# The gates of a mixture of experts loaded from ScalarE's queue, one expert sooner, and constant rows filled for one head and copied by transfers

## The chip, the cores and the metric

The kernel runs on one core of a Trainium2 chip. The core has TensorE (PE, matrix products; PEld is its weight load), VectorE (DVE), ScalarE (ACT), GpSimd (POOL) and SyncE (SP), each with its own queue of instructions taken in order, and DMA engines that move data between HBM and the on-chip memory SBUF and within SBUF. A transfer is started by an instruction in some engine's queue; SP does nothing else in this kernel. The metric is the time of one launch on the device in microseconds (us), lower being better.

## The reference, cut to what matters

Four blocks follow each other on an input of 4 sequences of 1024 tokens of 128 channels, each as `x = x + layernorm(block(layernorm(x)))`: an RWKV layer, a mixture of 16 experts with a shared one, a DeltaNet (linear attention), and a grouped-query attention with a mixture of 8 experts. The change touches the second and prepares the fourth.

```python
# second block: 4 of 16 experts by grouped top-k, and a shared one
weights, idx = _gate(x, w_gate)
combine = (one_hot(idx, E) * weights[..., None]).sum(1)          # [tokens, 16]
g = silu(einsum('th,efh->tef', x, w1_e))
u = einsum('th,efh->tef', x, w3_e)
routed = einsum('tef,ehf,te->th', g * u, w2_e, combine)
return routed + swiglu_shared(x)

# third block, per head and token: state M (8x8) and Z (8), decayed by beta
M = M * b_t + k_t v_t^T;  Z = Z * b_t + k_t
y_t = (q_t M) / (q_t Z + eps)

# fourth block: 16 query heads, 4 key heads of 8 channels, causal
att = softmax(q k^T / sqrt(8)); h = x + (att v) wo; out = h + moe8(rmsnorm(h))
```

## The kernel before, in words

Channels stand on the 128 partitions and tokens along the free axis. A sequence is worked in two halves of `CH` = 512 tokens, so most operations have the shape 128x512. Three overlapping stretches make up the span:

- **0 to 303 us.** The RWKV layer (`time_mixing`, `channel_mixing`, up to L355), and from about 190 us the first experts beside it.
- **190 to 683 us.** Experts (`gates_b` L382, `stage_b` L453) and from 303 us the first two sequences' DeltaNet (`stage_c` L551). The order in which a Python loop calls them is `with_experts`: a step of the DeltaNet adds 0.28 (a scan step) or 0.1 to a counter, and one step of the experts is called whenever it passes 1. Before this point a scheduler of the framework decides the order on each engine from the program, its dependencies and its buffers, so a line that waits for something else may change the order of many others.
- **683 us to the end.** Attention, the 8 experts and the DeltaNet of the last two sequences. Their order is written out by hand (`tc.manual_schedule()` near the end of the program).

**Experts.** Two experts of 64 hidden channels fill 128 partitions, so 16 experts are 8 pairs; from here "expert" means such a pair. For each half, `stage_b` goes through `[8 (shared), 0, 1, ..., 7]`. `begin(j)` issues: a product into PSUM; on DVE `x` = that, bounded below (L472); on ACT Exp, Ln, Exp, which make the sigmoid `g` (L474 to L476); for j < 8 the load of the gate and on POOL `x * gate` (L481); on POOL `g * x` (L482). Two experts later come the product `u_ps`, `g * u` on DVE (L492) and the product into `y_ps` (L465). The gates of a half are the rows of the combine weights, which `gates_b` computes on DVE (top-k) and writes to HBM (`rows`, L448). The load of an expert's gate (L480, on SP) reads its two rows from HBM and spreads each over 64 partitions: a tile 128x512 of 256 KB. Three buffers (`bufs=3`) hold gates, so the load of one waits until the multiply of the gate three back is done. There are 64 such loads (4 sequences, 2 halves, 8 experts).

**DeltaNet.** For each half `stage_c` loads the rotary table (`turn`, L570), computes `v`, writes it to HBM (`v_rows`, L582), makes `phi` for queries and keys (POOL `u` L599, DVE L603 and L610, ACT between), loads each value row spread over the partitions (`vrep`, L619, SP), multiplies it by the keys (POOL `kv`, L623), scans along time (DVE, L629, two scans for each of 9 rows), adds the two states (POOL `qs`, L639) and multiplies by the queries (DVE, L643). At the end POOL adds the result to the stream `xT` (L713).

**Attention's tiles.** `keys_r` (2 tiles, 2 halves x 4 heads of 512) and `queries_r` (2 tiles, 16 heads of 512) are bfloat16, heads along the free axis. Rows 0 to 71 are filled for each half by `spread` (L893) with 18 transfers (L901, L905) from `dk` and `dq` in HBM, where `heads` (L846) has written them (L883). Rows 64 to 127 hold constants first: -1 for keys, 0 for queries. Four memsets on POOL write them (L824, L825), in the program text just behind the first sequence's DeltaNet.

The lines that the change and the steps of the prediction touch most are `begin` in `stage_b` and the memsets.

Of the kernel before, what the change touches and what calls it, by code (L numbers as in the profile page):

```python
# [21 lines left out]
CH = 512  # L22
NH = T // CH
# [16 lines left out]
def sandwich(ctx: ExitStack, tc: tile.TileContext, x, vecs, cmats, rope, wa, wb, wc, wd, out):  # L40
# [3 lines left out]
    nc = tc.nc  # L44
# [69 lines left out]
    def chunk(h):  # L114
        return slice(h * CH, (h + 1) * CH)

    def rstd(var, eps, scale=1.0, to=None):

        r = var if to is None else to
        nc.scalar.activation(r, var, AF.Ln, bias=eps, scale=scale)  # L120
        nc.scalar.activation(r, r, AF.Exp, scale=-0.5)
        return r

    def mean_square(pp, src, bias=0.0):
        sq = pp.scratch("rs")
        nc.scalar.activation(sq, src, AF.Square, bias=bias)  # L126
        return project(pp, mean, sq, "ln_v")
# [8 lines left out]
    def project(pp, lhsT, rhs, name):  # L136
        ps = pp([P, CH], name)
        nc.tensor.matmul(ps, lhsT=lhsT, rhs=rhs, start=True, stop=True)  # L138
        return ps
# [313 lines left out]
    def stage_b(b, pp):  # L453

        n1, rows = ready_b.pop(b)
        pairs_of = rows.rearrange("(c e) k t -> c (e k) t", e=2)

        for h in range(NH):
            c = chunk(h)
            py = pp([P, CH], "y_ps")  # L460
            hid = []

            def add_up(last):
                w, a = hid.pop(0)
                nc.tensor.matmul(py, lhsT=w, rhs=a, start=(w is w2s), stop=last)  # L465

            def begin(j):


                pgate = project(pp, w1s if j == 8 else w1[:, j, :], n1[h], "g_ps")  # L470
                x = pb.tile([P, CH], FP, tag="x", name="x", bufs=3)
                nc.vector.tensor_scalar_max(x, pgate, -41.0)  # L472
                g = pb.tile([P, CH], FP, tag="g", name="g", bufs=4)
                nc.scalar.activation(g, x, AF.Exp, scale=-1.0)  # L474
                nc.scalar.activation(g, g, AF.Ln, bias=one)
                nc.scalar.activation(g, g, AF.Exp, scale=-1.0)  # L476
                if j < 8:

                    gate = pb.tile([P, CH], FP, tag="gate", name="gate", bufs=3)
                    nc.sync.dma_start(out=gate, in_=pairs_of[j][:, c].unsqueeze(1).to_broadcast([16, 8, CH]))  # L480
                    nc.gpsimd.tensor_mul(x, x, gate)  # L481
                nc.gpsimd.tensor_mul(g, g, x)  # L482
                return g

            begun = []
            for j in [8, 0, 1, 2, 3, 4, 5, 6, 7, None, None]:
                if j is not None:
                    begun.append((j, begin(j)))
                if len(begun) > 2 or j is None:
                    k, g = begun.pop(0)  # L490
                    pup = project(pp, w3s if k == 8 else w3[:, k, :], n1[h], "u_ps")
                    nc.vector.tensor_mul(g, pup, g)  # L492
                    hid.append((w2s if k == 8 else w2[:, k, :], g))
                if len(hid) > 1:
                    add_up(False)
                if j is not None:
                    yield
            add_up(True)
            rs = rstd(mean_square(pp, py), eps5, to=pp.scratch("rs"))
            nc.vector.tensor_mul(rs, py, rs)  # L500
            nc.gpsimd.tensor_add(xT[b][:, c], xT[b][:, c], rs)
            yield
# [224 lines left out]
    def experts_b(b):  # L727

        ahead = gates_b(b + 1, room_b) if b + 1 < NB else iter(())
        for n, _ in enumerate(stage_b(b, room_b)):  # L730
            if n in (3, 5) or 10 < n < 18:
                next(ahead, None)
            if n + 1 == 20:
                whole(ahead)
            yield
# [12 lines left out]
    while running or behind_a or coming_a:  # L748
        if coming_a and count >= BEHIND:
            b, h = coming_a[0]  # L750
# [5 lines left out]
        for item in list(running):  # L756
            kind, b, h, steps = item
# [63 lines left out]
    keys_r = [pk.tile([P, NH, 4, CH], BF, name=f"keys_r{i}") for i in range(2)]  # L821
    queries_r = [pe.tile([P, 16, CH], BF, tag=f"qr{i}", name=f"queries_r{i}", bufs=1) for i in range(NH)]
    for kr, qr in zip(keys_r, queries_r):
        nc.gpsimd.memset(kr[64:128], -1.0)  # L824
        nc.gpsimd.memset(qr[64:128], 0.0)  # L825

    def parts3(dst, src):

# [536 lines left out]
```

## Time and profile before

| | |
|---|---|
| median of 3 runs | 1573.81 us (1573.48 to 1579.96) |
| profiled execution | 1576.56 us, of it span 1574.8 us |
| mean granted TensorE clock | 0.892 |
| busy: PE / DVE / ACT / POOL | 78% / 68% / 54% / 53% |
| DMA engines | 59329 packets, 90.48 MB |

The profile is one execution as the hardware profiler saw it. Times in a timeline count from the start of the span. "L481" is line 481 of the kernel before; "x<-x,gate" says that tile x is written from x and gate. "SPq" is the queue of transfers on SP: a row of it is the issue of a transfer, not the transfer. In the timeline, brackets give the idle time ahead of an instruction on its engine, and what ended it. The granted clock is the share of its full speed that TensorE was given.

### The profile page before, as it was taken

The page shows a single profiled execution, that of the slowest core. Times are in us where ns is not written, and L with a number is a line of the kernel's source. Part 1 is how long each engine was busy: PE and PEld are TensorE (multiplying, and loading weights), DVE is VectorE, ACT ScalarE, POOL GpSimd, SP SyncE. Part 2 cuts the span into 40 slices and gives each one's busy share as a digit, 9 for nine tenths or more (in the row PEclk, how much of TensorE's full clock was granted, in tenths as well). Part 3 has the DMA queues.
Part 4 walks back from the last instruction along what each step waited for, and adds up shares of the span by engine and source line. Part 5 has one row for each costly group of instructions (what it writes and reads, how often), then busy time and mean ns, then how long its engine had stood idle before and what let it go on. Part 6 is the DMA issues. An engine that isn't in the chain of part 4 may idle for free.

```text
span 1574.8 us, 15028 instructions
## 1 busy us (share of the span) xinstructions
PE 1231.2 (78%) x4524; PEld 448.9 (29%) x4532; DVE 1064.7 (68%) x1755; ACT 849.2 (54%) x1565; POOL 842.2 (53%) x901
## 2 busy tenths in 40 slices
PE   3478889949878678888689778858977888989864
PEld 1123333313223223233223223312322333233211
DVE  4676775567864786876996896697479666577501
ACT  3566777544437445546445446534653474755541
POOL 5565485696838657953534653562556454223312
PEclk8677999968879789999889899988998999999986
DMA  2000020321223413201102111312121113111102
GB/s 105 14 14 0 14 69 32 73 72 48 93 40 98 137 40 100 67 28 59 50 30 87 50 42 44 103 49 74 56 83 38 57 38 105 44 59 45 57 24 61
DMA packets 59329, 90.48 MB, mean 57 GB/s; under 512 B 9904, under 2 KB 26800, under 8 KB 58544
## 3 DMA queue, kind: packets, MB, share of 16 engines
q1 hardware_dynamic: 59248, 89.52, 18.9%
q8 instruction: 36, 0.59, 0.2%
q14 instruction: 45, 0.37, 0.1%
HBM read 76.38 MB, written 12.71 MB: 57 GB/s over the span
## 4 chain that ended last, share of the span: by engine, by line
PE 35%; DVE 23%; ACT 7%; POOL 5%; issue 4%; SPq 2%; DMA 2%; POOLq 0%; DVEq 0%; ACTq 0%
DVE st L629 8%; PE av L992 7%; PE sc L1000 5%; DVE ms L936 4%; PE y L1131 3%; DVE ms L941 3%; PE ln_v L138 3%; PE sm L940 2%; PE sm L928 2%; ACT pr L1005 2%; PE g_ps L138 2%; DVE qs L643 2%; PE u_ps L138 1%; PE y_ps L465 1%; PE num_ps L680 1%
## 5 line engine op out<-in xcount | busy, mean ns | idle before, releaser
L1005 ACT ACTIVATE pr<-sc 128x512 f32<-128x512 f32 x576 | 328.4, 596 | 294.9 <-PE sc L1000 289.3
L936 DVE TENSOR_REDUCE ms<-sm 128x1 f32<-128x512 f32 (+3 forms) x352 | 212.3, 632 | 109.8 <-PE sm L932 101.7
L1000 PE MATMUL sc<-queries_r,keys_r 128*128 128x512 bf16 x576 | 224.6, 399 | 29.2 <-ACT pr L1005 27.6
L941 DVE TENSOR_REDUCE ms<-sm 128x1 f32<-128x512 f32 x256 | 166.0, 681 | 59.0 <-PE sm L940 58.9
L992 PE MATMUL av<-pr,va 128*32 128x512 f32 x1152 | 170.9, 652 | 4.2 <-POOL pr L1009 3.3
L928 PE MATMUL sm<-keys_r,queries_r 125*128 125x512 bf16 (+3 forms) x512 | 131.3, 313 | 44.9 <-DVE ms L936 37.1
L1009 POOL TENSOR_SCALAR_AFFINE_SELECT pr<-pr 128x512 f32<-128x512 f32 x128 | 95.4, 759 | 119.7 <-ACT pr L1005 119.0
L138 PE MATMUL ln_v<-rs,cm 128*128 128x512 f32 x176 | 110.1, 718 | 42.1 <-ACT rs L126 33.5
L1119 POOL TENSOR_TENSOR share<-n,every 128x512 f32<-128x512 f32 x64 | 80.6, 1273 | 99.5 <-DMA every<-row 58.5
L639 POOL TENSOR_TENSOR qs<-st,st 128x512 f32<-128x512 f32 x72 | 101.7, 1414 | 40.4 <-PE num_ps L680 15.6
L940 PE MATMUL sm<-keys_r,queries_r 125*128 125x512 bf16 x256 | 95.1, 395 | 22.8 <-DVE ms L941 19.5
L623 POOL TENSOR_TENSOR kv<-vrep,phi 128x512 f32<-128x512 f32 x64 | 86.7, 1357 | 41.7 <-issue 18.6
L481 POOL TENSOR_TENSOR x<-x,gate 128x512 f32<-128x512 f32 x64 | 84.0, 1314 | 46.7 <-ACT g L474 43.7
L482 POOL TENSOR_TENSOR g<-g,x 128x512 f32<-128x512 f32 x72 | 92.7, 1291 | 12.8 <-POOL x L481 6.7
L138 PE MATMUL g_ps<-n,wbt 128*128 128x512 f32 x144 | 83.8, 672 | 16.0 <-DVE x L472 7.5
L465 PE MATMUL y_ps<-g,wbt 128*128 128x512 f32 x144 | 79.7, 639 | 21.0 <-DVE g L492 20.6
L1000 PEld LDWEIGHTS <-keys_r 128*128 128x128 bf16 x576 | 57.5, 102 | 130.5 <-issue 101.5
L932 PE MATMUL sm<-later,identb 128*128 128x128 bf16 (+2 forms) x344 | 86.5, 251 | 0.0
L492 DVE TENSOR_TENSOR g<-u_ps,g 128x512 f32<-128x512 f32 x72 | 49.3, 685 | 54.7 <-POOL g L482 32.7
L138 PE MATMUL u_ps<-n,wbt 128*128 128x512 f32 x144 | 79.8, 638 | 1.7 <-DVE x L472 0.7
L928 PEld LDWEIGHTS <-queries_r 125*128 125x128 bf16 x512 | 48.6, 102 | 108.4 <-issue 91.5
L474 ACT ACTIVATE g<-x 128x512 f32<-128x512 f32 x72 | 45.0, 626 | 57.0 <-DVE x L472 56.9
(302 smaller groups left out, 2369.4 us busy)
## 6 DMA issues: line engine op xcount, KB each, us to landing
gate<-rows SPq DMA_DIRECT2D x64, 256.0 KB
vrep<-v_rows SPq DMA_DIRECT2D x64, 256.0 KB
every<-row SPq DMA_DIRECT2D x64, 256.0 KB
queries_r<-dq SPq DMA_DIRECT2D x72, 128.0 KB
turn<-in_rope_dram SPq DMA_DIRECT2D x8, 512.0 KB
dq<-qp SPq DMA_DIRECT2D x8, 384.0 KB
keys_r<-dk SPq DMA_DIRECT2D x72, 32.0 KB
sums<-av_sb SPq DMA_DIRECT2D x128, 18.0 KB
```

The source lines that it names most:

```text
L138: nc.tensor.matmul(ps, lhsT=lhsT, rhs=rhs, start=True, stop=True)
L465: nc.tensor.matmul(py, lhsT=w, rhs=a, start=(w is w2s), stop=last)
L629: nc.vector.tensor_tensor_scan(sts[e][i], beta[i], kvs[e], before if h else 0.0, op0=ALU.mult, op1=ALU.add,)
L639: nc.gpsimd.tensor_add(sums_e[e][0], s0, s1)
L928: nc.tensor.matmul(view[:, k, :], lhsT=qr[0:MROWS, h, tb], rhs=kr[0:MROWS, half, h // 4, 0:n_s], start=(k == 0), stop=False, skip_group_ch ...
L936: nc.vector.tensor_reduce(ms[:, 0, h0 : h0 + in_bank], view, AX.X, ALU.max)
L940: nc.tensor.matmul(sc, lhsT=qr[0:MROWS, h, tb], rhs=kr[0:MROWS, 0, h // 4, :], start=True, stop=True)
L941: nc.vector.tensor_reduce(ms[:, 1, h : h + 1], sc, AX.X, ALU.max)
L992: nc.tensor.matmul(pavs[b, i][32 * g : 32 * g + 32, :], lhsT=va[:, j, g, :], rhs=pr, start=(j == 0), stop=(j == i),)
L1000: nc.tensor.matmul(sc, lhsT=kr[0:ROWS, j // 4, g, j % 4 * P : (j % 4 + 1) * P], rhs=qr[0:ROWS, 4 * g : 4 * g + 4, tb], start=True, stop=True,)
L1005: nc.scalar.activation(pr, sc, AF.Exp)
L1009: nc.gpsimd.affine_select(out=every, in_=every, compare_op=ALU.is_ge, fill=0.0, base=0, pattern=[[0, 4], [1, P]], channel_multiplier=-1,)
```

## The change

1. The load of a gate moves from SP's queue to ACT's, and each expert loads the gate of the next one: the shared expert (8) loads that of expert 0, expert 0 that of expert 1, and so on; expert 7 loads none. The number of loads, their size and the number of buffers stay. A list `gates` carries the tile from one `begin` to the next.
2. The memsets fill rows 64 to 127 for one head only (64x512 in place of 64x4096 and 64x8192). Four transfers on SP copy this head to the other 15 query heads or 7 key heads, within SBUF.

```diff
                 if j < 8:
+                    nc.gpsimd.tensor_mul(x, x, gates.pop(0))
+                if j != 7:
 
                     gate = pb.tile([P, CH], FP, tag="gate", name="gate", bufs=3)
-                    nc.sync.dma_start(out=gate, in_=pairs_of[j][:, c].unsqueeze(1).to_broadcast([16, 8, CH]))
-                    nc.gpsimd.tensor_mul(x, x, gate)
+                    nc.scalar.dma_start(
+                        out=gate, in_=pairs_of[(j + 1) % 9][:, c].unsqueeze(1).to_broadcast([16, 8, CH])
+                    )
+                    gates.append(gate)
                 nc.gpsimd.tensor_mul(g, g, x)
                 return g
 
-            begun = []
+            begun, gates = [], []
...
     for kr, qr in zip(keys_r, queries_r):
-        nc.gpsimd.memset(kr[64:128], -1.0)
-        nc.gpsimd.memset(qr[64:128], 0.0)
+
+        nc.gpsimd.memset(kr[64:128, 0, 0, :], -1.0)
+        nc.gpsimd.memset(qr[64:128, 0, :], 0.0)
+        first, others = qr[64:128, 0:1, :], qr[64:128, 1:16, :]
+        nc.sync.dma_start(out=others, in_=first.to_broadcast([64, 15, CH]))
+        kf = kr.rearrange("p a b t -> p (a b) t")
+        first, others = kf[64:128, 0:1, :], kf[64:128, 1 : NH * 4, :]
+        nc.sync.dma_start(out=others, in_=first.to_broadcast([64, NH * 4 - 1, CH]))
```

## The prediction

> **What bounds the kernel now.** I read the busy shares first, then the table of stretches, then the timelines of POOL, VectorE (DVE) and SyncE (SP) around the lines that the diff touches, and last the chain that ended last.
>
> ```profile
> PE 1231.2 (78%) x4524; PEld 448.9 (29%) x4532; DVE 1064.7 (68%) x1755; ACT 849.2 (54%) x1565; POOL 842.2 (53%) x901
> PE 35%; DVE 23%; ACT 7%; POOL 5%; issue 4%; SPq 2%; DMA 2%; POOLq 0%; DVEq 0%; ACTq 0%
> 250.00:300.00 50.00, 45.60 (x115) 17.80 (x114) 29.96 (x66) 35.16 (x65) 26.92 (x22) 1.00 0.15 42
> 300.00:350.00 50.00, 28.69 (x52) 9.59 (x50) 27.79 (x32) 21.26 (x41) 49.03 (x36) 0.80 0.30 83
> 350.00:400.00 50.00, 41.29 (x82) 13.33 (x82) 37.80 (x52) 23.82 (x48) 31.02 (x26) 0.83 0.23 72
> 500.00:550.00 50.00, 32.79 (x59) 10.97 (x58) 31.30 (x41) 24.14 (x49) 33.41 (x29) 0.80 0.46 142
> ```
>
> The first line is busy time, the second the shares of the chain, the others stretches (length, then busy PE, weight loads, DVE, ACT, POOL, granted clock, DMA share, GB/s). Over the whole span TensorE (PE) leads and POOL is half idle; but from 300 to 350 us POOL is busy 49.03 of 50 us while PE does 28.69 and is granted 0.80. POOL's timeline says why:
>
> ```profile
> 303.56 3.51 POOL L824 MEMSET keys_r<- 64x4096 bf16 x1
> 310.92 6.92 POOL L825 MEMSET queries_r<- 64x8192 bf16 x1
> 317.92 1.26 POOL L599 TENSOR_TENSOR u<-u,w 128x512 f32<-128x512 f32 x1
> 319.24 3.51 POOL L824 MEMSET keys_r<- 64x4096 bf16 x1
> 322.69 7.20 POOL L825 MEMSET queries_r<- 64x8192 bf16 x1
> 329.97 1.27 POOL L599 TENSOR_TENSOR u<-u,w 128x512 f32<-128x512 f32 x1
> 339.19 2.48 POOL L623 TENSOR_TENSOR kv<-vrep,phi 128x512 f32<-128x512 f32 x2
> ```
>
> Columns: start, duration, engine, line, tiles. The four memsets (21.1 us) stand in front of the two `u` sums, from which DVE makes `phi`, from which the scans and `kv` of the first DeltaNet half start. DVE's and PE's timelines show the same stretch:
>
> ```profile
> 319.22 3.81 DVE L603 TENSOR_SCALAR w<-u 128x512 f32<-128x512 f32 x1 [3.72 <-POOL u L599]
> 324.83 4.11 PE L138 MATMUL g_ps<-n,wbt 128*128 128x512 f32 x4 [6.07 <-ACT rs L120]
> 348.00 2.07 PE L669 MATMUL den_ps<-qs,cm 128*128 128x512 f32 x2 [9.78 <-DVE qs L643]
> ```
>
> In brackets: idle time before, and who ended it. L603 takes 0.43 us elsewhere and 3.81 beside a memset. Now the gates: SP's waits, its own order in the second sequence's DeltaNet, and the multiply there.
>
> ```profile
> SPq L480 <- POOL x L481: 218.5, 50, 26.9
> 520.55 0.60 SPq L905 DMA_DIRECT2D queries_r<-dq  x1
> 521.19 0.59 SPq L480 DMA_DIRECT2D gate<-rows  x1
> 521.83 1.87 SPq L619 DMA_DIRECT2D vrep<-v_rows  x3
> 526.33 1.26 POOL L481 TENSOR_TENSOR x<-x,gate 128x512 f32<-128x512 f32 x1 [2.78 <-DMA gate<-rows]
> 528.89 2.49 POOL L623 TENSOR_TENSOR kv<-vrep,phi 128x512 f32<-128x512 f32 x2
> ```
>
> SP stands 218.5 us waiting for a gate buffer to come free, which costs SP nothing by itself. In the whole trace POOL's multiply is late for its gate once, by 2.78 us: there the gate's issue stood behind 18 spreading transfers. Elsewhere the idle time ahead of that line is ended by ScalarE (ACT), as the page's row of it shows:
>
> ```profile
> L481 POOL TENSOR_TENSOR x<-x,gate 128x512 f32<-128x512 f32 x64 | 84.0, 1314 | 46.7 <-ACT g L474 43.7
> L474 ACT ACTIVATE g<-x 128x512 f32<-128x512 f32 x72 | 45.0, 626 | 57.0 <-DVE x L472 56.9
> ```
>
> **What can move.** In the two built programs the orders agree on all engines up to the first gate (about 190 us) and in the part whose order is written out (683 us to the end). So 190 to 683 changes; the 892 us behind it move as a block.
>
> **The change by parts**, against the profiled execution: 1576.56 us, span 1574.8 and 1.8 around it, 2.75 above the median of 1573.81. I add the sum to the median.
>
> *Memsets and copies.* One 512-wide row of 4096 is an eighth of a key memset and of 8192 a sixteenth of a query memset: (3.51 + 3.51) / 8 + (6.92 + 7.20) / 16 = 1.8 us, so POOL loses 19.4 us of 21.1. SP issues four copies, at 0.6 each 2.4 us; together 2 x (15 + 7) x 64 = 2816 packets of 1 KB. The page's 59248 packets took 18.9% of 16 engines for 1574.8 us, 0.080 each, so 2816 x 0.080 / 16 = 14.1 us of all engines, while the DMA share there is 0.30. The first user is the first spreading transfer (495.1 us), 170 us later: hidden. On the path: `u` would come 5 us sooner (317.9 to 312.6) and `kv` about 17 sooner (339.2 to about 322), as the built order puts both `u` and the first `kv` directly behind the short memsets. But three experts that before ran ahead of or beside the memsets now stand behind the scans, at 2.5 to 3.7 us each (a multiply, a second one of 1.27, and the hand-overs); 3 x 3.7 = 11. I take -17 + 11 = -6, bounds -17 and 0.
>
> *Gate issues on ACT, 190 to 303.* 18 of the 64 fall here, at the 0.515 us of the SP rows: 9.3 us more on ACT, which idles 29.5 of 110 us between 190 and 300 (busy 45.32 + 35.16). Each waits in ACT's queue for the multiply of the expert three back, since there are three buffers. Behind it stand Exp, Ln and the RWKV layer's activations, and PE (45.60 of 50 busy) waits for those. In this part the waited-for multiply is two experts old. +2; bounds 0 (all in the idle) and +9.
>
> *Gate issues on ACT, 303 to 508.* In the built order of ACT many issues stand between the Ln and the last Exp of the very expert whose multiply frees the buffer. That is a loop: multiply 1.27, issue 0.52, Exp 0.6, second multiply 1.27, with semaphores about 4.0 us per expert, against 2.5 where experts stand back to back on POOL now (550.86 to 553.43). If 20 experts lost 1.5 each it would be 30; but most share POOL with the scans' `kv` and `qs`, which fill the gaps. +4; bounds 0 and +10.
>
> *Second sequence's DeltaNet, 508 to 683.* The gate is no longer behind the 18 transfers: the 2.78 us goes, and DVE's wait behind it. But the built program puts eight whole experts, and the top-k chain for the next gates, ahead of the `kv` of this half; and some SP transfers (spreading, `v_rows`, with `vrep` behind them) now wait for completions of gate transfers, with which they share a semaphore. Eight experts at 4.0 to 4.5 are 32 to 36 us, so `kv` goes from 528.89 to about 563. Those experts were run later before, beside the scans: 17 POOL operations, 21.6 us, come off there, and about 4 of PE and DVE time. 34 - 21.6 - 4 = 8, and of the some 26 issues left (13 us on ACT) I leave 2 on the path. I take +10; bounds -14 (POOL's idle pieces of 2.47, 4.44, 4.30 and 2.78 us in 508 to 526 all filled) and +35 (nothing regained).
>
> Sum: -6 + 2 + 4 + 10 = **+10, so 1584 us**.
>
> **Two rules beside the rows.** The trace shows a gate late once (2.78 us in 64). The Trainium skill, DMA: Bandwidth & Descriptors, "Issuing engines are not separate DMA queues", says that issuing from several engines saves only the sequencer's issue time; by it the move is worth at most the 18 x 0.65 = 12 us of queueing seen here. The same page's anatomy of a DMA adds that a semaphore wait is taken on the issuing sequencer; the waits of 218.5 us that were harmless on SP would then stand on ACT, and the rule speaks against the change. On DVE, L603 was 3.81 us beside a memset; SBUF — State Buffer, "Who interferes with whom", has POOL and DVE's tensor_scalar exclude each other, by which 3.4 us goes with the memset; that is already inside my 17.
>
> **The rivals.** *Faster:* the memsets are the bound of 300 to 350, ACT's idle takes the issues, and the experts placed behind the scans fill POOL's gaps: -17 - 2.78 = -20, about 1554. For it: 49.03 of 50 busy, PE idle 6.07 and 9.78. Against: PE's clock and the following stretch (PE 41.29 of 50) leave little room to catch up experts. It decides as soon as the costs of the three other parts stay below 9 of the 17. *Much slower:* the cross waits hold: eight experts of 4.0 ahead of `kv` and nothing regained, -6 + 2 + 4 + 35 = +35, about 1609. For it: `kv` is waited for by every scan. Against: POOL has 16.6 us idle in 500 to 550 to regain work with. *Nothing:* gates were in time and the manual part hides a shift, about 1574. Against: 683 us starts with the last addition of stage B, no slack.
>
> **How the numbers follow.** Forecast 0.45 (1575 to 1600, that is -6 + 0 + 0 + 7 to +26), faster rival 0.32 (1545 to 1566), much slower 0.15 (1600 to 1625), nothing 0.08. Within 0.5% (7.9 us, about what a measurement of this kernel can tell from no change: 1566 to 1582) lie a quarter of the forecast (0.11), 0.02 of the faster rival and 0.06 of nothing, 0.19. Faster: 0.30 + 0.02 = 0.32. Slower: 0.34 + 0.15 = 0.49. Both signs hold most of the chance, so the range is wide: cutting a quarter of the faster rival and two thirds of the much slower one (0.08 + 0.10) leaves 1551 to 1610. The forecast's own range is 1575 to 1600.
>
> **What would show it.** Memsets of 0.3 to 0.5 us instead of 3.5 to 7, L603 at 0.43, and the first `kv` near 322 show the first part; if the first DeltaNet half (its last addition at 386.2 now) does not end 6 us sooner, the experts took it back. ACT's waits on the gate line, absent now, show the loops: over 40 us of them with PE idle behind, and the forecast stands; a few us, and the faster rival does. The first `kv` after the second spreading near 563, and the first scores at 682.3 moved by +10, show the last part. I am wrong if that half starts its `kv` before 540, or if the loops stay below 3 us per expert.

## The result

The changed kernel takes 1585.9 us (median of 6 runs, 1581.47 to 1588.55) against 1574.69 for the kernel before beside it: a ratio of 1.0062, with a 95% interval of 1.0043 to 1.0081. It is slower by 0.6%. Measured once more beside another kernel, the ratio was 1.0058 (1.0043 to 1.0072). The profiled execution took 1581.47 us, the lowest of its six, with a span of 1579.6 us; that of the repetition took 1584.49.

The page of the changed kernel, first the busy shares and then those of the chain that ended last:

```profile
PE 1235.2 (78%) x4532; PEld 447.3 (28%) x4532; DVE 1055.6 (67%) x1755; ACT 847.1 (54%) x1565; POOL 823.8 (52%) x901
PE 29%; DVE 14%; ACT 5%; POOL 4%; issue 3%; DMA 2%; SPq 1%; POOLq 0%; ACTq 0%; DVEq 0%
```

POOL lost 18.4 us of work (842.2 to 823.8) and DVE 9.1, ACT 2.1; PE got 4.0 more. The engines together work less, so the loss is in waiting. The table of stretches of the changed kernel, same columns as before:

```profile
300.00:350.00 50.00, 36.26 (x63) 11.05 (x64) 35.80 (x46) 20.17 (x45) 37.27 (x43) 0.80 0.62 151
500.00:550.00 50.00, 34.16 (x83) 13.87 (x81) 30.95 (x69) 25.78 (x45) 24.37 (x20) 0.86 0.31 95
550.00:600.00 50.00, 31.86 (x55) 8.59 (x56) 32.46 (x39) 14.34 (x36) 33.46 (x28) 0.83 0.30 89
```

From 300 to 350 POOL is no longer full (37.27 us, 49.03 before) and PE does 36.26 in place of 28.69: the memsets' gain. From 500 to 600 PE does 66.0 in place of 73.6, and POOL 57.8 in place of 58.9, of which only 24.4 in the first half: there the time is given back. Rows picked from POOL's timeline of the changed kernel show both places:

```profile
310.17 0.52 POOL L829 MEMSET keys_r<- 64x512 bf16 x1
311.17 0.52 POOL L830 MEMSET queries_r<- 64x512 bf16 x1
319.27 1.26 POOL L603 TENSOR_TENSOR u<-u,w 128x512 f32<-128x512 f32 x1 [0.84 <-DVE w L596]
327.12 2.50 POOL L627 TENSOR_TENSOR kv<-vrep,phi 128x512 f32<-128x512 f32 x2 [1.93 <-DVE phi L614]
...
512.44 1.27 POOL L505 TENSOR_TENSOR xT<-xT,rs 128x512 f32<-128x512 f32 x1 [1.28 <-DVE rs L504]
516.18 1.28 POOL L478 TENSOR_TENSOR x<-x,gate 128x512 f32<-128x512 f32 x1
541.83 1.27 POOL L478 TENSOR_TENSOR x<-x,gate 128x512 f32<-128x512 f32 x1 [10.37 <-ACT g L474]
559.17 1.27 POOL L505 TENSOR_TENSOR xT<-xT,rs 128x512 f32<-128x512 f32 x1 [7.64 <-DVE rs L504]
562.26 1.27 POOL L486 TENSOR_TENSOR g<-g,x 128x512 f32<-128x512 f32 x1 [1.82 <-ACT g L476]
563.49 2.51 POOL L627 TENSOR_TENSOR kv<-vrep,phi 128x512 f32<-128x512 f32 x2
```

The first `kv` of all comes at 327.12 (339.19 before). The first `kv` of the second sequence comes at 563.49 (528.89 before): from 512 to 562 POOL works through eight experts alone, with idle pieces of 10.37 and 7.64 us.

Followed at fixed points of the program (start of the instruction, us, from the timelines of POOL):

| point | before | changed | difference | grown by |
|---|---|---|---|---|
| last addition of the RWKV layer (L355) | 301.78 | 307.16 | +5.4 | +5.4 |
| end of the first DeltaNet half (L713; L717 in the changed kernel) | 386.18 | 378.37 | -7.8 | -13.2 |
| end of its second half | 467.81 | 456.36 | -11.4 | -3.6 |
| last addition of the experts (L501; L505 in the changed kernel) | 682.30 | 685.58 | +3.3 | +14.7 |
| end of the span | 1574.8 | 1579.6 | +4.8 | +1.5 |

The spans differ by 4.8 us, the medians by 11.2: the profile of before ran 1.9 us above its median and that of the changed kernel 4.4 below. In the profile of the repetition the same steps are +6.4, -13.2, -3.8, +16.6 and +1.6, together +7.6.

### The profile page after: what moved, and what is told of

The parts are those of the page before. It is cut to its first block, busy times and chain, and to the rows that moved or that the text cites. A ratio compares the mean times of both kernels' runs of the same rounds, so it can differ in the third digit from the quotient of the medians.

```text
span 1579.6 us, 15053 instructions
## 1 busy us (share of the span) xinstructions
PE 1235.2 (78%) x4532; PEld 447.3 (28%) x4532; DVE 1055.6 (67%) x1755; ACT 847.1 (54%) x1565; POOL 823.8 (52%) x901
## 2 busy tenths in 40 slices
DMA packets 62210, 93.37 MB, mean 59 GB/s; under 512 B 9969, under 2 KB 29681, under 8 KB 61425
## 3 DMA queue, kind: packets, MB, share of 16 engines
q1 hardware_dynamic: 52912, 75.63, 16.6%
## 4 chain that ended last, share of the span: by engine, by line
PE 29%; DVE 14%; ACT 5%; POOL 4%; issue 3%; DMA 2%; SPq 1%; POOLq 0%; ACTq 0%; DVEq 0%
PE av L1002 7%; PE sc L1010 5%; DVE st L633 4%; DVE ms L946 3%; DVE ms L951 3%; PE y L1141 3%; PE sm L950 2%; PE sm L938 2%; ACT pr L1015 2%; PE ln_v L138 2%; DMA every<-row 1%; PE num_ps L684 1%; PE sm L942 1%; POOL pr L1019 1%; POOL qs L643 1%
## 5 line engine op out<-in xcount | busy, mean ns | idle before, releaser
L1002 PE MATMUL av<-pr,va 128*32 128x512 f32 x1152 | 174.1, 659 | 3.0 <-POOL pr L1019 3.0
L643 POOL TENSOR_TENSOR qs<-st,st 128x512 f32<-128x512 f32 x72 | 100.4, 1397 | 34.3 <-PE num_ps L684 17.5
L942 PE MATMUL sm<-later,identb 128*128 128x128 bf16 (+2 forms) x352 | 90.2, 256 | 0.0
L465 PE MATMUL y_ps<-g,wbt 128*128 128x512 f32 x144 | 75.9, 609 | 7.9 <-DVE g L496 7.9
L472 DVE TENSOR_SCALAR x<-g_ps 128x512 f32<-128x512 f32 x72 | 49.2, 685 | 48.5 <-PE g_ps L138 48.4
```

The lines of the kernel that those rows point to most:

```text
L643: nc.gpsimd.tensor_add(sums_e[e][0], s0, s1)
L942: nc.tensor.matmul(view[:, :, n_s - P :], lhsT=identb, rhs=later[:, :in_bank, :], start=False, stop=True, skip_group_check=True,)
L1002: nc.tensor.matmul(pavs[b, i][32 * g : 32 * g + 32, :], lhsT=va[:, j, g, :], rhs=pr, start=(j == 0), stop=(j == i),)
```

## The experiments

The question is which part pays and where. Theory A: the copies gain, and the gates lose because they leave SP's queue, which shows at the second sequence's first `kv`. The rivals stand in the expectations.

**1. The copies alone.** Of the change only the second part:

```diff
-        nc.gpsimd.memset(kr[64:128], -1.0)
-        nc.gpsimd.memset(qr[64:128], 0.0)
+        nc.gpsimd.memset(kr[64:128, 0, 0, :], -1.0)
+        nc.gpsimd.memset(qr[64:128, 0, :], 0.0)
+        ... the four copies on SP
```

> Only the memsets and copies of the change; gates from SP as before. Theory A (what the change loses, it loses because gates leave SP's queue, and this shows in the first half of the second sequence's DeltaNet): the first kv of the first DeltaNet half near 322 to 327 us (339.2 before, 327.1 after), its end near 375 (386.2), the first kv of the second sequence near 517 (528.9 before, 563.5 after), the stretch to 683 ends 8 to 13 us sooner, ratio to before 0.992 to 0.995. Rival B (the memsets' gain is taken back later by the experts left over, whatever the gates do): ratio 0.999 to 1.003, with the last addition of the experts within 3 us of 682.3.

1564.03 us, ratio 0.9922 (0.9901 to 0.9942). POOL's timeline of this kernel:

```profile
311.00 1.26 POOL L599 TENSOR_TENSOR u<-u,w 128x512 f32<-128x512 f32 x1 [0.84 <-DVE w L592]
320.04 2.49 POOL L623 TENSOR_TENSOR kv<-vrep,phi 128x512 f32<-128x512 f32 x2 [2.07 <-DVE phi L610]
```

`kv` starts 19.2 us sooner than before. The first half ends at 374.28 (-11.9), the second at 451.96 (-15.9), the second sequence's first `kv` comes at 511.80 (-17.1) and the experts' last addition at 664.58 (-17.7). Of each of these differences 1.7 us stand there before the change can act (last RWKV addition 300.13, 301.78 before). Nothing of the gain is taken back before the hand-ordered part, and rival B falls. In this profile that part is 5 us longer than in the one of before (897.6 against 892.5 us from the last addition to the end; in the other runs it takes 893.7 to 896.9). Why is not settled.

**2. The gates alone.** The first part of the change with the long memsets.

```diff
-                    nc.sync.dma_start(out=gate, in_=pairs_of[j]...)
+                    nc.scalar.dma_start(out=gate, in_=pairs_of[(j + 1) % 9]...)
```

> Only the gates of the change (ACT's queue, one expert sooner); the long memsets stay. Theory A: the first kv of the second sequence near 570 (12 us of the memsets on top of 563.5, at most), the experts' last addition near 695, ratio 1.010 to 1.016. Rival B: as after, 1.004 to 1.008.

1607.29 us, ratio 1.0203 (1.018 to 1.0226): more than expected. The second sequence's first `kv` comes at 587.13 and the experts' last addition at 709.21, 26.9 us later than before. With the gates on ACT the short memsets are worth more (23.6 us at that addition, 709.21 to 685.58) than alone (17.7).

**3. The whole change, the gates still on SP.**

```diff
-                    nc.scalar.dma_start(
+                    nc.sync.dma_start(
                         out=gate, in_=pairs_of[(j + 1) % 9]...
```

> The whole change, but the gate's load stays in SP's queue (still one expert sooner). Theory A: the eight experts ahead of the second sequence's first kv are gone, that kv near 517, ratio as with the copies alone, 0.992 to 0.996. Rival C (being one expert sooner is what costs: a gate holds its buffer for longer): 1.004 to 1.008, as after.

1566.32 us, ratio 0.9933 (0.991 to 0.9956), like the copies alone; the second sequence's first `kv` is at 516.80. One expert sooner costs nothing that these runs can tell, and rival C falls. It does not help either: in SP's queue the gate still stands behind the spreading, and POOL waits 3.19 us for it once.

**4. The copies, and each expert's own gate from ACT.**

```diff
-                    nc.sync.dma_start(out=gate, in_=pairs_of[j]...)
+                    nc.scalar.dma_start(out=gate, in_=pairs_of[j]...)
```

> The copies, and the gates from ACT's queue, but each expert loads its own gate as before. Theory A: as after, the first kv of the second sequence near 563, ratio 1.004 to 1.010. Rival C: as the copies alone, 0.992 to 0.996. A third reading (loading sooner is what keeps ACT's waits short): multiplies on POOL wait 2 to 3 us for each gate, 64 times, ratio above 1.03.

1589.96 us, ratio 1.0105 (1.0072 to 1.0137), slightly above the top of the expected range; first `kv` of the second sequence at 570.39. The queue costs, with or without "sooner". The third reading falls too: without "sooner" POOL's multiply waits for a gate 2 times, 2.9 us together.

**5 and 6. Which gates.** The whole change with the queue chosen by sequence, first all but the third from ACT, then the third alone:

```diff
-                    nc.scalar.dma_start(
+                    (nc.sync if b == 2 else nc.scalar).dma_start(      # 5
+                    (nc.scalar if b == 2 else nc.sync).dma_start(      # 6
```

> The whole change, but the 16 gates of the third sequence (those whose experts stand beside the second sequence's DeltaNet) stay in SP's queue; the other 48 come from ACT. Theory A (what is lost is lost where those experts are placed ahead of the second sequence's kv): that kv near 520, the experts' last addition between 668 and 676, ratio 0.994 to 0.999, above the 0.9933 of all gates on SP only by the 5 us that the gates cost before 307. Rival D (each issue on ACT costs its part, whatever stands behind it): three quarters of the loss between 0.9933 and 1.0062 remain, 1.003.

> The reverse: only the 16 gates of the third sequence come from ACT, the other 48 from SP. Theory A: the second sequence's first kv near 558, ratio 1.000 to 1.005. Rival D: a quarter of the loss, 0.9965, that kv near 520.

Run 5: 1571.55 us, 0.9965 (0.9955 to 0.9976), `kv` at 516.14. Run 6: 1573.65 us, 0.9984 (0.9972 to 0.9997), `kv` at 563.19. Sixteen gates move `kv` by 47 us, forty-eight others do not move it: place, not number, decides, and for `kv` rival D falls. For the time it is not so clear: run 6 lies below the range of theory A (1.000 to 1.005) and above rival D's 0.9965, and the forty-eight are not free. Against run 3 the profiled spans grow by 6.3 us (run 5) and 7.6 us (run 6), and nothing of the 6.3 is left from the early part, since at the end of the second DeltaNet half run 5 stands at 456.17 and run 3 at 456.59. The third half takes 2.2 us more, and 4.7 lie in the fourth sequence, from the end of the third half to the experts' last addition: 96.4 us in run 5 and 91.8 in run 3. ACT's waits in that stretch (waited for, us, times, longest), run 5:

```profile
ACT g L476 <- POOL x L478: 16.6, 6, 3.4
ACT g L474 <- DVE x L472: 6.7, 6, 3.2
ACT g L474 <- DMA gate<-rows: 4.1, 1, 4.1
```

and run 3, where the first and the third kind do not occur:

```profile
ACT g L474 <- DVE x L472: 16.2, 11, 3.2
```

The first row is the loop of the prediction: the gate's issue stands between Ln and the last Exp, and ACT waits up to 3.4 us for POOL. That it makes the 4.7 us fits, but was not shown: the wait for a gate's transfer (4.1) is new too, and the wait for DVE is shorter by 9.5.

**7 and 8. The spreading called later.** In the whole change, and then in the copies alone:

```diff
     for h in range(NH):
         with_experts(heads(0, h))
-        whole(spread(0, h))
     with_experts(stage_c(1, room_c, pp_q))
+    for h in range(NH):
+        whole(spread(0, h))
```

> The whole change, all gates from ACT, but the 36 spreading transfers of the first sequence are called after the second sequence's DeltaNet and no longer between its v and its kv. Theory A, in the form that the experts run ahead of kv because kv waits for values that stand behind the spreading on SP: the first kv of the second sequence comes before 515, the experts' last addition near 672, ratio 0.990 to 0.999. Rival E (with the gates on ACT the experts go ahead whatever SP does): that kv stays near 560, ratio 1.004 to 1.009.

> The copies alone (gates on SP as before) with the same later spreading. If the 12 us of spreading ahead of vrep (493 to 505 us) are on the path there: the first kv of the second sequence near 498 in place of 511.8, ratio 0.984 to 0.990, the fastest so far. If the experts and scans take that time anyway, or the first maxima wait for the late spreading: 0.991 to 0.996.

Run 7: 1571.85 us, 0.9969 (0.9955 to 0.9983). All 64 gates come from ACT, and yet POOL's timeline has the second sequence's first `kv` right behind the end of the previous experts:

```profile
513.38 1.26 POOL L505 TENSOR_TENSOR xT<-xT,rs 128x512 f32<-128x512 f32 x1 [0.90 <-DVE rs L504]
514.60 1.27 POOL L627 TENSOR_TENSOR kv<-vrep,phi 128x512 f32<-128x512 f32 x1
```

Rival E falls: in all these runs the eight experts go ahead only where the values of `kv` stand behind the spreading in SP's queue and the gates of their sequence do not. Run 8: 1562.47 us, 0.9909 (0.9895 to 0.9923), between the two ranges expected and not told apart from the copies alone. Its `kv` starts at 507.14 (511.80 in run 1), but the half ends at 573.85 (572.82): the 12 us of spreading ahead of `vrep` are hidden.

**9. The whole change once more.** No edit.

> The whole change once more, beside the next kernel on one chip, since its ratio (1.0062) is higher than what the two parts of the gates' move come to when each is added to the change with all gates on SP: 0.9933 + 0.0032 + 0.0051 = 1.0016. If the parts add, 0.9995 to 1.004 here; if something more is lost only when all 64 gates come from ACT, 1.005 to 1.008 again.

1584.89 us, 1.0058 (1.0043 to 1.0072). Against run 3 that is 1.25%, where runs 5 and 6 add up to 0.83%. In the profiled spans they add up to 13.9 us of 14.6 (the first profile) or 17.4 (this one). By the ratios, which were taken on three chips, some 0.4% is lost only when all gates come from ACT, just beyond the scatter of four intervals; where, stays open. So of the 1.25% that the move to ACT costs, 0.51 go with the sixteen gates that make `kv` late.

**10. All gates on SP, one expert sooner, spreading later.** The edits of runs 3 and 7 together.

> The whole change with all gates on SP (still one expert sooner), and the first sequence's spreading called after the second's DeltaNet. If a gate issued one expert sooner is of use at all, it is here, where spreading no longer stands ahead of gates in bulk: 0.987 to 0.990, below the 0.9909 of the copies with late spreading. If gates were in time anyway: 0.990 to 0.993.

1560.35 us, 0.9901 (0.9883 to 0.9919), the lowest of all, but not told apart from runs 8 and 1. POOL waits for no gate in either of runs 8 and 10, so "sooner" has nothing left to remove.

**11. Wait or order.** In the changed kernel two things stand ahead of the late `kv`. One is the order on POOL. The other is a hold on SP, seen in its waits between 478 and 548 us and in its queue (spreading L911 and L915, `v_rows` L586, `vrep` L623):

```profile
SPq L915 <- DMA gate<-rows: 28.5, 3, 21.1
...
501.95 0.60 SPq L911 DMA_DIRECT2D keys_r<-dk  x1
523.67 0.60 SPq L915 DMA_DIRECT2D queries_r<-dq  x1
...
532.57 0.45 SPq L586 DMA_DIRECT2D v_rows<-v  x1
545.80 1.88 SPq L623 DMA_DIRECT2D vrep<-v_rows  x3
```

A spreading transfer reads and writes nothing of a gate, yet it waits for one for 21.1 us (and the key transfers, L911, for 8.8 in 4 pieces): in the built program transfers from SP and ACT take turns on the same eight completion semaphores, and whoever takes one waits for its last user. `v_rows`, at 496.55 in run 3, goes out at 532.57. Run 11 issues the gates from POOL, whose transfers have semaphores of their own:

```diff
-                    nc.scalar.dma_start(
+                    nc.gpsimd.dma_start(
```

> The whole change, but the gates' loads are issued from POOL's queue, whose transfers have completion semaphores of their own, in place of ACT's. In the built order the eight experts still stand ahead of the second sequence's first kv. If the hold of SP (28.5 us of spreading waiting for gates that it does not need, in the trace of after) is what makes kv late: SP waits for no gate, vrep is issued before 520 and kv starts by 530. If the order on POOL is enough by itself: vrep is issued before 520 just the same, but kv still starts after 550, behind the eighth expert. The time itself says little, since issuing costs POOL an unknown amount for each of 64 gates: 0.995 to 1.02.

1602.59 us, 1.0152 (1.0127 to 1.0176); an issue takes POOL 0.54 us, and no row of SP's waits there names a gate. SP's and POOL's timelines of this kernel:

```profile
523.12 1.87 SPq L623 DMA_DIRECT2D vrep<-v_rows  x3
...
560.06 1.27 POOL L478 TENSOR_TENSOR x<-x,gate 128x512 f32<-128x512 f32 x1 [10.61 <-PE u_ps L138]
580.79 1.27 POOL L486 TENSOR_TENSOR g<-g,x 128x512 f32<-128x512 f32 x1 [1.82 <-ACT g L476]
582.02 2.50 POOL L627 TENSOR_TENSOR kv<-vrep,phi 128x512 f32<-128x512 f32 x2
```

`vrep` is issued at 523.12 (3 us later than expected), DVE writes `phi`, the other operand, at 521.95, and from 530 to 535 the DMA engines stand still (share 0.00). So nothing that `kv` reads was late, but it starts at 582.02, behind the eighth expert. The order on POOL is enough to make `kv` late; the hold on SP is real and does not decide it. What the hold would cost under another order was not tried.

## Why the prediction was right, and where it was not

**The sum.** +10 was forecast, 1584 us; the medians differ by 11.2 and, in the repetition, 10.5. All four terms were mis-sized, the third beyond its bounds, and the errors partly cancel: together they come to +3.3 and +6.0 in the two profiles, and to +4.8 and +7.6 with the hand-ordered part. What is left to the medians lies in how each profiled execution stands to its own. The sign and the place of the loss were foreseen; that the sum comes so near is in part luck.

| term of the sum | forecast | profile after | repetition |
|---|---|---|---|
| gate issues on ACT, 190 to 303 | +2 (0 to +9) | +5.4 | +6.4 |
| memsets and copies, to the end of the first half | -6 (-17 to 0) | -13.2 | -13.2 |
| gate issues on ACT, to the end of the second half | +4 (0 to +10) | -3.6 | -3.8 |
| second sequence's DeltaNet | +10 (-14 to +35) | +14.7 | +16.6 |

**Memsets and copies.** `kv` was to come "about 17 sooner", and this held: counted from the last RWKV addition it comes 17.5 us sooner both in the changed kernel and in run 1 (20.0 and 19.9 us behind that addition, 37.4 before). L603 (L607 in the changed kernel) takes 0.833 us at most, 3.81 before, and the Trainium skill's statement in SBUF — State Buffer, "Who interferes with whom", that POOL and DVE's tensor_scalar can exclude each other, agrees with that. ("0.43 us elsewhere" left out a second one of 1.47 at 331.28, beside POOL's addition at 331.20.) The page counts 62210 DMA packets, 2881 more, where 2816 were worked out; the DMA share from 300 to 350 doubles to 0.62 and no computing engine waits for it. The step that failed is "three experts ... now stand behind the scans ...; 3 x 3.7 = 11". They do stand there, but counted as above the half ends 13.2 us sooner in the changed kernel and 10.2 in run 1, so the three took 4.3 and 7.3 us. In run 1 most of that comes back too: at the experts' last addition 16.1 of the 17.5 are kept. The three filled gaps of POOL, as the faster rival had it.

**Gate issues on ACT, early.** Every run with the first sequences' gates off SP reaches the last RWKV addition at 305.3 to 309.2, every run with them on SP at 300.1 to 302.0. The size is inside the bounds, but the working is not shown: ACT waits for POOL's multiply there for only 2.4 us (1.2 twice), so it is the issues or the changed order behind them, and the runs do not part these. The delay arises between two additions of that layer, at 254.90 and 289.75 (255.14 and 283.77 before). In run 11, where ACT issues no gate but POOL does, the last addition is as late (305.87), so issues on ACT are not needed for it. By the end of the second half the difference is gone (run 5 and run 3).

**Gate issues on ACT, 303 to 508.** The loops were to cost 4; this stretch got shorter by 3.6, as it did in run 1 without them (4.0). The loops exist. In the whole trace of the changed kernel ACT has

```profile
ACT g L476 <- POOL x L478: 23.4, 11, 3.5
```

and 12.7 us of it, in 6 pieces, lie between 303 and 508; 9.4 lie behind the third half's end. Two experts that follow each other so on POOL (353.97, 357.85, 362.03) take 3.9 and 4.2 us, as forecast. The step that failed is that these waits reach the path. The forecast had named over 40 us of them for its case and a few us for the faster rival; it was between. The shortening goes with the clock: from the end of the first half to that of the second TensorE was granted 0.89 (run 1: 0.91) in place of 0.81, and the same 133 matmuls took 59.8 us (58.2) in place of 65.6. At 0.89 to 0.91 this stretch takes 0.2 to 0.3 us more with all gates on ACT (the changed kernel, runs 7 and 9) than with all on SP (1 and 8); at 0.81 to 0.84 it takes 1.7 to 3.8 more (2 and 4 against before, 3 and 10). What sets the clock here is not shown.

**Second sequence's DeltaNet.** This step carries the result. `kv` was to come "from 528.89 to about 563"; it came at 563.49, behind eight experts. That this moment fits is luck too: counted from the end of the second half, which had moved by -11.4, `kv` is 46.1 us later, where 34 were forecast. The regained time was to be 21.6 + 4; it was 31.3, of which 9.2 up to the end of the third half and 22.1 behind it. So the eight experts took 5.8 us each and not 4.0 to 4.5, with POOL idle for the 10.37 and 7.64 us of the timeline. The first of the two is the top-k chain for the next gates, which the forecast named and gave no price: ACT stands still until the chain's product is there.

```profile
538.69 0.57 ACT L447 COPY comb<-comb_ps 16x512 f32<-16x512 f32 x1 [8.63 <-PE comb_ps L445]
```

In the kernel before POOL has the same idle piece, but behind the last `qs` of this half (570.49):

```profile
582.12 1.27 POOL L481 TENSOR_TENSOR x<-x,gate 128x512 f32<-128x512 f32 x1 [10.37 <-ACT g L474]
```

So this wait was not new. It moved ahead of `kv` with the experts and came off later, which fits that more was lost and more regained than forecast. The cause was put on the built order and on the shared semaphores alike; run 11 shows that the order suffices.

**The rivals.** The faster one, 1554, is close to run 1, which leaves the gates' move out (1564.03, or 12.5 below its own kernel before): its mechanism held there, with 12.5 us in place of 20, and its condition, costs of the other parts below 9 us, did not. In the much slower one the regained time was to be nothing; 31 us were regained. "Nothing" had the part ordered by hand hide a shift; it hid none here (+3.3 us at its start, +4.8 at its end).

**The two rules.** The Trainium skill's DMA: Bandwidth & Descriptors, "Issuing engines are not separate DMA queues", has the move save only issue time. Runs 3 and 10 agree: gates from SP are in time (at most 3.2 us of waiting in 64 loads), and none of the kernels with gates on another queue is faster than its partner on SP. The waits for a free buffer did move into ACT's queue, but only in part: the 23.4 us above, against 218.5 on SP before.

## What to carry to other kernels

Before a transfer is moved to another queue, ask what its old place held back. Here a gate's load behind the spreading held the experts back for just the time in which `kv` could not run either; without it a scheduler placed eight experts ahead of the chain that everything waits for. Judge the two halves of such a change apart: 0.8% was gained by the copies and more than all of it lost by the queue.

## What the runs showed of the hardware and the program that was not expected

- A transfer can wait for one that it shares no data with: 28.5 us on SP for gates issued by ACT, through shared completion semaphores; with the gates issued by POOL, which use others, no such wait is left (run 11).
- Issuing the 128x512 gate takes 0.515 us on SP, 0.522 on ACT and 0.54 on POOL; a memset of 64x512 bfloat16 takes 0.52 us on POOL, where an eighth of 64x4096 (3.51) would be 0.44.
- Taking the long memsets off POOL was worth more with the gates on ACT (23.6 us at the experts' last addition) than with them on SP (17.7). Why was not looked into.
